# FP4 block in an order written out by hand, one PSUM tile for each gate product, and moved fillers in the attention passes

## The chip, the cores and the metric

The kernel runs on one core of one Trainium2 chip. The metric is the time of one execution on the device in microseconds (us), lower is better. Engines are named as in the profile: PE (TensorE, matrix products into PSUM), DVE (VectorE), ACT (ScalarE), POOL (GpSimd), SP (SyncE, which issues the DMAs).

## The reference

Two layers work on `x` of shape (8, 224, 512) with a context `ctx` of shape (8, 750, 512), all in float32. Each layer is a gated cross attention and a gated feed-forward block. Cut to what matters:

```python
x = x + tanh(g_xattn[0]) * xattn16(layernorm(x), ctx)      # 16 heads of 32
x = x + tanh(g_ffn[0])   * ternary_ffn(layernorm(x))       # 512 -> 2048 -> 512
x = x + tanh(g_xattn[1]) * xattn8(layernorm(x), ctx, mask) # 8 heads of 64, masked
x = x + tanh(g_ffn[1])   * fp4_ffn(layernorm(x))           # 512 -> 1408 -> 512

def bit_linear(x, w):             # ternary_ffn: two of these, with a convolution of
    return einsum(act_quant(x), weight_quant(w))   # three taps and silu between them

def fp4_quant_dequant(x):         # blocks of 16
    scale = max(|x|) / 6
    return nearest of (0, .5, 1, 1.5, 2, 3, 4, 6) to |x / scale|, * sign(x) * scale

def fp4_ffn(x):
    gate, y = fp4_linear(x, w_gate), fp4_linear(x, w_up)
    return fp4_linear(silu(gate) * y, w_down)
```

## The kernel before

The work is cut into sixteen passes, `n` from 0 to 15, and a block at the end. Passes 0 to 7 are the eight batches of the first layer's attention (`attention16`), passes 8 to 15 those of the second layer's (`attention8`). The FP4 feed-forward block (`ffn1`) then works on 14 tiles of 128 rows; tiles 0 and 1 have their hidden part computed inside pass 15 (`ffn1_head`), so the block computes the hidden part of tiles 2 to 13 and the output of all 14.

**Queues of pieces.** Matrix work that no pass waits for at once is written as generators that yield after every matmul or small group, each time with its cost on PE and on DVE: the keys and queries of the next pass (`keys_queries`), the values (`values`), the projections of the pass before (`project_out`, `ffn0_out`), the ternary feed-forward (`ffn0`), the FP4 quantization of the weights (`fp4_weights`, lines 959 to 974 and 1000) and of the activations (`fp4_steps`). `fill(us, queues)` issues pieces until that much PE time is covered; `pace(us, queue)` issues pieces until DVE has that much to do. `self.owed` is the PE time already covered beyond what was asked, `self.behind` the DVE time put behind.

**First layer.** A pass has sixteen slots of scores and maxima: scores in the PSUM tile `quad` (line 461), a maximum on DVE (line 468), and `fill(1.72)` for PE meanwhile. Then come twelve steps: scores again (429, 438), the exponential on ACT (504), filler of 2.05, DVE work of up to 4.0, in which a ternary product (813, into bank `t`) may lie, and the products with the values (515). A reciprocal and a product (524, 525) close each group of three steps. `diagonals` and `spread` (193, 201, 204) lay the ternary scale `bc` over the partitions ahead of the ternary products; line 821 takes a product out of bank `t` into `hp`.

**Second layer.** A pass has eight slots: scores (612), the masked maximum (623), the exponential (644), products with the values (575) and transposes of the weights (670, copied at 675). `divided` turns the row sums into reciprocals in steps: rows `stat` on DVE (586 to 411), their transposes (417) with a copy to `sT` (419), a product that spreads them (593, copied at 597), and a product on DVE (601). The transposes of the FP4 weights (1000, copied at 1018 or 1028), of `stat` and of the normalized rows `xn` (185, copied at 186) all go through the one buffer of PSUM bank `t`; keys (293, copied to `kT` at 302), queries, values and projections share the two buffers of bank `m`.

**FP4 block.** `ffn1_hidden` takes four chunks of 352 columns. For each, four matmuls make the gate product, ACT a tanh and DVE `gth` (1078), four more make the up product, and DVE multiplies (1080). Both products are halves of one PSUM tile, `ps_big`, of which there are two. `ffn1_in` loads a tile `xf`, normalizes it, quantizes it (POOL has the last step, 974) and transposes it into `xqT` (1055; copied by `evac`, in turn on ACT, line 89, and on DVE, line 91). `ffn1_out` transposes the quantized hidden row (1092, copied at 1093), multiplies with `wd` (1097) and stores (1109, 1110).

**Order.** `pin` makes PE, DVE and ACT follow the order in which the kernel's lines were traced. Here it is called ahead of the FP4 block, so the block's order is a scheduler's, and its lines only say what depends on what; a dependency is kept by tile, not by part of a tile.

## Time and profile before

| | |
|---|---|
| median of 3 runs | 2239.82 us (2235.03 to 2239.95) |
| the profiled execution | 2234.42 us, span 2232.6 us |
| PE busy | 2151.8 us, 96% |
| DVE busy | 1385.0 us, 62% |
| ACT busy | 699.2 us, 31% |
| POOL busy | 130.7 us, 6% |
| DMA queue of the program | 79.18 MB, 11.3% of 16 engines |
| first layer's passes 2 to 7 | 124 us each, PE busy 121.3 |
| second layer's passes 10 to 13 | 97 to 98 us each, PE busy 93.8 to 95.4 |
| FP4 block, 1829 to 2229 | 400 us, PE busy 391.4 |

A float32 matmul stands in the trace as two records, a float32 transpose as one. A group of records is given with its start, its length, the line and the tiles, and in brackets the idle time of the engine ahead of it with what ended it. Times inside a pass are from the span's start. The granted clock is the share of TensorE's full clock that the throttle let through.

### The profile page before, as it was taken

How to read it: one execution, taken by the hardware profiler on the slowest of the kernel's cores; microseconds unless marked ns; L12 is line 12 of the kernel's file. 1: busy time of each engine (PE TensorE's matmuls, PEld its weight loads, DVE VectorE, ACT ScalarE, POOL GpSimd, SP SyncE). 2: the span in 40 equal slices, each digit the busy share in tenths (PEclk: the TensorE clock that was granted, in tenths of full speed). 3: DMA queues.
4: the chain of work that ended last, by engine and by line, in shares of the span. 5: the costliest groups of instructions: out<-in, count | busy, mean ns of one | idle time of the engine just before them, and what ended most of it. 6: DMA issues, size and time to landing. Idle time of an engine off the chain costs nothing.

```text
span 2232.6 us, 33189 instructions
## 1 busy us (share of the span) xinstructions
PE 2151.8 (96%) x14062; PEld 1226.2 (55%) x14062; DVE 1385.0 (62%) x2618; ACT 699.2 (31%) x1173; POOL 130.7 (6%) x145
## 2 busy tenths in 40 slices
PE   7989899999999999999899999999999999999999
PEld 4444546364555546465656565665656555555554
DVE  3786767676766767773656565564523468666652
ACT  1222415151423325152543343343434321110111
POOL 0000000000000000000001010110000012111110
PEclk9999999999999999999999999999999999999999
DMA  6210010101000011101011212122110020000000
GB/s 218 67 38 29 1 45 2 31 15 30 16 18 29 7 39 39 63 2 63 3 38 57 63 28 64 41 67 66 37 36 15 9 85 10 5 20 19 19 5 19
DMA packets 48628, 81.30 MB, mean 36 GB/s; under 512 B 3296, under 2 KB 27616, under 8 KB 48352
## 3 DMA queue, kind: packets, MB, share of 16 engines
q1 hardware_dynamic: 48480, 79.18, 11.3%
q8 instruction: 110, 1.80, 0.3%
q14 instruction: 38, 0.31, 0.0%
HBM read 65.28 MB, written 13.89 MB: 35 GB/s over the span
## 4 chain that ended last, share of the span: by engine, by line
PE 84%; DVE 12%; ACT 2%; issue 1%; DMA 1%; SPq 0%; POOL 0%; ACTq 0%; DVEq 0%
PE ps_m L354 14%; PE ps_m L293 12%; PE ps_big L1066 7%; PE ps_pa L515 6%; PE ps_m L1097 6%; PE ps_m L378 5%; PE ps_quad L461 4%; PE ps_half L612 4%; PE ps_m L322 4%; PE ps_half L670 4%; PE ps_pa L575 4%; PE ps_quad L438 3%; PE ps_t L813 2%; DVE part L468 2%; PE ps_m L1066 2%; PE ps_quad L429 1%
## 5 line engine op out<-in xcount | busy, mean ns | idle before, releaser
L293 PE MATMUL ps_m<-cx,wk 128*128 128x375 f32 x1024 | 362.4, 487 | 10.0 <-DMA wk<-in_L_Wk 10.0
L354 PE MATMUL ps_m<-wv,cx 128*125 128x512 f32 x768 | 354.5, 602 | 0.0
L623 DVE CUSTOM_DVE_ANT_0 ps_half<-ps_half,mbias 112x750 f32<-112x750 f32 x128 | 121.1, 946 | 292.1 <-PE ps_half L612 291.8
L468 DVE TENSOR_REDUCE part<-ps_quad 112x4 f32<-112x1500 f32 x128 | 220.0, 1719 | 127.0 <-PE ps_quad L461 127.0
L293 PEld LDWEIGHTS ps_m<-cx,wk 128*128 128x128 f32 x1024 | 182.4, 191 | 110.8 <-issue 28.3
L354 PEld LDWEIGHTS ps_m<-wv,cx 128*125 128x125 f32 x768 | 136.1, 187 | 173.8 <-issue 168.8
L504 ACT ACTIVATE p<-ps_quad 125x1792 f32<-125x1792 f32 x96 | 159.7, 1664 | 198.8 <-PE ps_quad L438 198.8
L363 ACT COPY v<-ps_m 125x512 f32<-125x512 f32 x96 | 56.1, 585 | 439.0 <-PE ps_m L354 433.8
L1097 PE MATMUL ps_m<-wd,hqT 128*128 128x512 f32 x308 | 138.3, 595 | 3.8 <-ACT hqT L1093 3.1
L644 ACT ACTIVATE p<-ps_half,nm 112x750 f32<-112x750 f32 x128 | 113.1, 888 | 47.6 <-DVE nm L635 41.7
L675 ACT COPY p<-ps_half 125x672 f32<-125x672 f32 x128 | 85.8, 722 | 131.6 <-PE ps_half L670 131.6
L461 PE MATMUL ps_quad<-kT,qT 32*112 32x375 f32 x1024 | 115.3, 519 | 11.8 <-DVE part L468 11.8
L378 PE MATMUL ps_m<-wo,aT 128*112 128x512 f32 x256 | 120.4, 601 | 0.0
L1066 PE MATMUL ps_big<-wg,xqT 128*128 128x352 f32 x352 | 115.4, 463 | 1.8 <-DVE h L1080 1.4
L1066 PE MATMUL ps_big<-wu,xqT 128*128 128x352 f32 x352 | 113.7, 466 | 0.8 <-DVE gth L1078 0.8
L837 DVE SCALAR_TENSOR_TENSOR y<-hp,cw,y 128x224 f32<-128x224 f32 x256 | 109.5, 449 | 4.5
L322 PE MATMUL ps_m<-xnT,wq 128*128 128x224 f32 x512 | 107.9, 357 | 0.6 <-ACT xnT L186 0.6
L515 PE MATMUL ps_pa<-p,v 125*32 125x224 f32 x1536 | 93.3, 361 | 14.8 <-ACT p L504 14.8
L1077 ACT ACTIVATE gth<-ps_big 128x352 f32<-128x352 f32 x48 | 22.2, 463 | 257.2 <-PE ps_big L1066 234.1
L670 PE MATMUL ps_half<-ident,p 112*125 112x112 f32 x768 | 99.9, 280 | 0.0
L612 PE MATMUL ps_half<-kT,qT 64*112 64x375 f32 x512 | 98.5, 498 | 0.9 <-ACT p L675 0.9
L322 PEld LDWEIGHTS ps_m<-xnT,wq 128*128 128x128 f32 x512 | 93.7, 190 | 9.4 <-issue 5.3
(199 smaller groups left out, 2873.7 us busy)
## 6 DMA issues: line engine op xcount, KB each, us to landing
cx<-in_ctx SPq DMA_DIRECT2D x32, 750.0 KB, 4.3
wst<-in_w SPq DMA_DIRECT2D x16, 512.0 KB, 7.8
x<-in_x SPq DMA_DIRECT2D x8, 448.0 KB, 7.0
mid<-x SPq DMA_DIRECT2D x8, 448.0 KB, 3.1
x<-mid SPq DMA_DIRECT2D x8, 448.0 KB, 3.5
last<-x SPq DMA_DIRECT2D x8, 448.0 KB, 3.1
out<-yout SPq DMA_DIRECT2D x14, 256.0 KB, 2.0
wraw<-in_w_gate SPq DMA_DIRECT2D x11, 256.0 KB, 2.6
```

Source lines behind the costliest of these rows:

```text
L293: nc.tensor.matmul(pk, lhsT=self.w["wk"][:, k, g * 128 : (g + 1) * 128], rhs=job["cx"][c][:, k, :], start=k == 0, stop=k == KC - 1,)
L322: nc.tensor.matmul(pq[:, g - g0, :], lhsT=self.w["wq"][:, k, g * 128 : (g + 1) * 128], rhs=xnT[:, k, :], start=k == 0, stop=k == KC - 1,)
L354: nc.tensor.matmul(pv, lhsT=job["cx"][c][:, k, at : at + CP], rhs=self.w["wv"][:, k, :], start=k == 0, stop=k == KC - 1,)
L378: nc.tensor.matmul(po, lhsT=aT[:, g, i * TP : (i + 1) * TP], rhs=self.w["wo"][:, g, :], start=g == 0, stop=g == KC - 1,)
L461: nc.tensor.matmul(sc[:, h, :MH], lhsT=qT[r, g, i * TP : (i + 1) * TP], rhs=kT[g][r, c * MH : (c + 1) * MH], start=True, stop=True,)
L468: nc.vector.tensor_reduce(part[:, i, g, :, c], sc[:, :, :MH], AX.X, ALU.max)
L504: nc.scalar.activation(p, pw[:, :, : 2 * S], AF.Exp)
L515: nc.tensor.matmul(pa[r, which, :], lhsT=self.ones[:CP, r] if which else job["v"][j][:, col : col + 32], rhs=p[:, h, (j - j0) * S : (j - j ...
L612: nc.tensor.matmul(sc[h][:, c, :MH], lhsT=qT[r, g, i * TP : (i + 1) * TP], rhs=kT[g][r, c * MH : (c + 1) * MH], start=True, stop=True,)
L670: nc.tensor.transpose(pt[:, j // half, j % half * TP : (j % half + 1) * TP], p[:, h, j * CP : (j + 1) * CP], self.ident[:TP, :TP],)
L1066: nc.tensor.matmul(ps[:, :CW], lhsT=xqT[:, k, :], rhs=wt[:, k, c0 : c0 + CW], start=k == 0, stop=k == KC - 1,)
L1097: nc.tensor.matmul(po, lhsT=hqT[:, k, :], rhs=wd[:, k, :], start=k == 0, stop=k == NC1 - 1)
```

## The change

- `transposed` takes a bank: the transposes of the queries' rows go to `m` in place of `t` where the queries' pass is 8 or later.
- In `attention16` the first slot's filler is 2.9 in place of 1.72 (not in pass 0), and the filler of 2.05 is less by 0.8 where the piece that `pace` will issue next is a ternary product (`ahead`, `self.coming`).
- In `attention8` the transposes of `stat` at slot 4 are traced ahead of the FP4 pieces; in pass 15, from slot 2, `pace` asks for 2.5 in place of 3.5.
- The last steps of a pass's reciprocals (`rest`) are issued together with every second matmul of the next pass's values, in one piece, in place of a piece of their own behind it.
- `xqT` is always copied by ACT. In `ffn1_head` the second tile's `xqT` has a buffer of its own, and the steps of the next tile's `ffn1_in` come after every fourth matmul in place of every fifth.
- In the FP4 block gate and up product have a PSUM tile each (`big=4`), and the loop over tiles writes out the order: while a tile's hidden part runs, the next tile's `ffn1_in`, the quantization of the tile before and the output of the tile before that are placed between its matmuls. `pin` is called at the very end, so this order holds on PE, DVE and ACT.

```diff
-        pt = self.ps("t", [128, KC, TP], BF16 if half else F32)
+        pt = self.ps(bank, [128, KC, TP], BF16 if half else F32)
...
+    def ahead(self, us, queue):
+        return self.coming if queue and self.behind < us else 0
...
-            self.transposed(xnT, xn, i)
+            self.transposed(xnT, xn, i, "t" if n < B else "m")
...
-                        self.fill(1.72, early, late)
+                        self.fill(2.9 if n and (g, i, c) == (0, 0, 0) else 1.72, early, late)
...
-                self.fill(2.05, late)
+                self.fill(2.05 - self.ahead(4.0 if j0 + 2 < NKT else 0.5, beside), late)
...
+            if slot == 4:
+                next(first)
             if not soon:
                 self.pace(1.5, beside)
-            if slot == 4:
-                next(first)
...
-                self.pace(3.5, beside)
+                self.pace(3.5 if n + 1 < 2 * B or slot < 2 else 2.5, beside)
...
         self.spread(bc, diags)
+        self.coming = 0.8
...
+            self.coming = 0.8 if g + 1 < ng else 0
             yield (0.8 if g < ng else 0), dve, g < ng
...
-        self.evac(xqT, pt)
+        nc.scalar.copy(xqT, pt)
...
         transposes(0, 4, "th")
         transposes(4, 8, "t")
+        yield
+        transposes(8, NC1, "th")
+        yield
         po = self.ps("m", [TF, D])
-        products(0, 4)
-        transposes(8, NC1, "th")
-        products(4, NC1)
+        products(0, 5)
+        yield
+        products(5, NC1)
...
-        room = self.att.tile([128, KC, MH], F32, name="cx", bufs=2)
+        room, other = (self.att.tile([128, KC, MH], F32, name="cx", bufs=2) for _ in range(2))
...
+        xqTs = [h["xqT"], other, h["xqT"]]
...
-                if i % 5 == 2 and i < 25:
+                if i % 4 == 2 and i < 27:
                     yield next(ahead)
...
         def banks():
-            ps = self.ps("big", [TF, 2, 512])
-            return ps[:, 0, :], ps[:, 1, :]
+            return [self.ps("big", [TF, CW]) for _ in range(2)]
...
+                ahead = self.ffn1_in(pool, f + 1, xf, xn, xT, 2)
+            steps = quantized(last)
+            for i, _ in enumerate(
+                self.ffn1_hidden(
+                    xqT, h, lambda: pool.tile([TF, CW], F32, name="gth", bufs=2), banks
+                )
             ):
+                if f + 1 < NF and i in (1, 4, 6, 9, 12, 14):
+                    next(ahead)
+                if i in (10, 15, 17, 20, 22, 25):
+                    next(steps)
+                if i in (23, 27):
+                    next(out)
+            for _ in steps:
                 pass
+            waiting.append(self.ffn1_out(pool, f, x, h, wd))
+            next(out)
...
-                for k, cost in enumerate(values):
-                    yield cost
+                for k, (pe, dve) in enumerate(values):
                     if k % 2:
-                        yield next(ends, (0, 0))
+                        more = next(ends, (0, 0))
+                        pe, dve = pe + more[0], dve + more[1]
+                    yield pe, dve
...
-        self.pin()
...
-            self.psum_pool(last, big=2, th=1)
+            self.psum_pool(last, big=4, th=1)
...
             self.ffn1(self.pool(last, "ffn1", side="right"), wd)
+            self.pin()
```

More of the change, by code (lines that the diff above doesn't have):

```diff
@@ L176, in normed, with transposed @@
         return xn
-    def transposed(self, dst, src, i):
+    def transposed(self, dst, src, i, bank="t"):
         nc = self.nc
         half = src.dtype == BF16
-        pt = self.ps("t", [128, KC, TP], BF16 if half else F32)
+        pt = self.ps(bank, [128, KC, TP], BF16 if half else F32)
         ident = self.ident16 if half else self.ident
@@ L1145, in quantized @@
                 yield from self.fp4_steps(work, part, part, part.shape[1])
+        other = other.rearrange("p k m -> p (k m)")[:, :D].rearrange("p (k t) -> p k t", k=KC)
+        xqTs = [h["xqT"], other, h["xqT"]]
         for f in range(2):
-            ahead = self.ffn1_in(there, f + 1, h["x"][f + 1], h["xn"], h["xqT"], 1)
+            ahead = self.ffn1_in(there, f + 1, h["x"][f + 1], h["xn"], xqTs[f + 1], 1)
             for i, cost in enumerate(
                 self.ffn1_hidden(
-                    h["xqT"],
+                    xqTs[f],
                     h["h"][f],
@@ L1169, in quantized @@
             for c0 in range(0, HID1, QW):
-                self.fp4(pool, h[:, c0 : c0 + QW], h[:, c0 : c0 + QW], QW, 2)
+                yield from self.fp4_steps(pool, h[:, c0 : c0 + QW], h[:, c0 : c0 + QW], QW, 2)
         def banks():
-            ps = self.ps("big", [TF, 2, 512])
-            return ps[:, 0, :], ps[:, 1, :]
+            return [self.ps("big", [TF, CW]) for _ in range(2)]
         x, h, xqT = self.head["x"], self.head["h"], self.head["xqT"]
-        waiting = [(0, x[0], h[0]), (1, x[1], h[1])]
@@ L1178, in ffn1 @@
-        x = x[2]
-        quantized(h[1])
+        waiting = [self.ffn1_out(pool, f, x[f], h[f], wd) for f in range(2)]
+        x, last = x[2], h[1]
         for f in range(2, NF):
+            out = waiting.pop(0)
             h = pool.tile([TF, HID1], F32, name="h", bufs=3)
-            for _ in self.ffn1_hidden(
-                xqT, h, lambda: pool.tile([TF, CW], F32, name="gth", bufs=2), banks
-            ):
-                pass
-            waiting.append((f, x, h))
+            if f + 1 < NF:
+                xf = pool.tile([TF, D], F32, name="xf", bufs=5)
+                xn = pool.tile([TF, D], F32, name="xn1", bufs=2)
+                xT = pool.tile([128, KC, TF], F32, name="xqT1", bufs=2)
+                ahead = self.ffn1_in(pool, f + 1, xf, xn, xT, 2)
[4 more added lines that the diff above has]
+                )
+            ):
+                if f + 1 < NF and i in (1, 4, 6, 9, 12, 14):
[5 more added lines that the diff above has]
+            for _ in steps:
+                pass
+            waiting.append(self.ffn1_out(pool, f, x, h, wd))
+            next(out)
@@ L1187, in ffn1 @@
             if f + 1 < NF:
-                x = pool.tile([TF, D], F32, name="xf", bufs=5)
-                xn = pool.tile([TF, D], F32, name="xn1", bufs=2)
-                xqT = pool.tile([128, KC, TF], F32, name="xqT1", bufs=2)
-                for _ in self.ffn1_in(pool, f + 1, x, xn, xqT, 2):
-                    pass
-            quantized(h)
-            self.ffn1_out(pool, *waiting.pop(0), wd)
-        for tile_ in waiting:
-            self.ffn1_out(pool, *tile_, wd)
+                for _ in ahead:
+                    pass
@@ L1200, in run @@
+                x, xqT = xf, xT
+            else:
+                for _ in quantized(h):
+                    pass
+                next(waiting[0])
+            for _ in out:
+                pass
+            last = h
+        first, second = waiting
+        next(first)
+        next(first)
+        next(second)
+        for _ in first:
+            pass
+        next(second)
+        for _ in second:
+            pass
     def run(self):
@@ L1202, in run @@
         self.setup()
-        self.owed, self.behind, self.jobs, self.w = 0, 0, {}, {}
+        self.owed, self.behind, self.coming, self.jobs, self.w = 0, 0, 0, {}, {}
         self.copy = self.nc.scalar.copy
```

## The prediction

> **What bounds the kernel now.** I read the page's busy times and its chain first, then the list of waits for TensorE alone, then the order in time around each wait.

> ```profile
> PE 2151.8 (96%) x14062; PEld 1226.2 (55%) x14062; DVE 1385.0 (62%) x2618; ACT 699.2 (31%) x1173; POOL 130.7 (6%) x145
> PE 84%; DVE 12%; ACT 2%; issue 1%; DMA 1%; SPq 0%; POOL 0%; ACTq 0%; DVEq 0%
> ```

> TensorE is busy 96% and is the chain. Its work is not changed, so only its waits can be won: 2232.6 - 2151.8 = 81 us, 10 of them the first load. The waits, as total, times, longest:

> ```profile
> PE ps_pa L515 <- ACT p L504: 14.8, 11, 1.9
> PE ps_quad L461 <- DVE part L468: 11.8, 16, 2.1
> PE ps_t L185 <- ACT wsome L1028: 2.5, 4, 0.7
> PE ps_m L1066 <- DVE wv L1078: 2.4, 2, 2.2
> PE ps_t L417 <- DVE hp L821: 2.2, 1, 2.2
> ```

> They are many, short and regular, so each place is looked at once and counted.

> **First layer, passes 1 to 7.** TensorE at the end of pass 2 (start, us, what; in brackets the idle time before it):

> ```profile
> 390.91 0.90 PE L293 MATMUL ps_m<-cx,wk 128*128 128x375 f32 x2
> 392.83 0.96 PE L515 MATMUL ps_pa<-p,v 125*32 125x224 f32 x16 [1.03 <-ACT p L504]
> ...
> 394.49 0.90 PE L461 MATMUL ps_quad<-kT,qT 32*112 32x375 f32 x8
> 395.31 1.93 PE L919 MATMUL ps_t<-w,hs 128*112 128x512 bf16 x8
> 398.29 0.90 PE L461 MATMUL ps_quad<-kT,qT 32*112 32x375 f32 x8 [1.04 <-DVE part L468]
> ```

> Filler ran out: one key matmul (two records, 0.63) stood where the exponential takes 1.66. Then the next pass's first maximum (1.71) came behind the reciprocal and product (1.56 + 0.39) with 1.93 of filler. In the built order of the changed kernel four key matmuls leave the early steps and two of them stand in the last one (three matmuls, 1.89, cover 1.66), and the first slot has twenty `L919` matmuls (4.3) instead of eight. Both waits go: -1.03 - 1.04. Given back: at step 1 the ternary product waits for `bc`, copied behind the exponential at 332.99 to 333.33 in pass 2; with 0.63 less ahead of it, its wait of 0.19 becomes 0.82 (+0.63). And one slot has two key matmuls (1.26) where a value and a key matmul stood (1.49), whose wait of 0.27 grows by 0.23. Net -1.2 in each of passes 2 to 7, -7.1. In pass 1 the wait of 2.10 at 152.4 and one of 0.62 at 206.7 are covered, 0.63 is given back, and the last steps stay short of filler: -2.5 (between 0 and -4).

> Edit against: the queries' transposes take bank `m` from `n >= B`, but the queries of layer 1's first pass run inside pass 7. There a key group has just ended in `m`, and the next needs its buffer: two buffers, transposes in the other. The copy `kT` comes behind the exponential, a tanh and two `y` on ACT and ended at 965.37, while the next key matmul started at 963.85. It will wait 1.5 us, and 1.7 at the second transposes: +3.2 (0 if ACT is early). Layer sum: -7.1 - 2.5 + 3.2 = -6.4.

> **Second layer, passes 8 to 14.** TensorE in pass 10:

> ```profile
> 1281.28 0.66 PE L1000 MATMUL ps_t<-ident,wq 128*128 128x128 f32 x4
> 1282.61 0.26 PE L417 MATMUL ps_t<-ident,stat 112*128 112x112 bf16 x2 [0.67 <-ACT wg L1018]
> ...
> 1292.36 0.66 PE L1000 MATMUL ps_t<-ident,wq 128*128 128x128 f32 x4
> 1293.69 0.60 PE L185 MATMUL ps_t<-ident,xn 112*128 112x112 f32 x4 [0.68 <-ACT wg L1018]
> ```

> One bank `t` is handed from the FP4 transposes to the next user through an ACT copy. A wait costs its idle time and about 0.2 of a weight load that no longer hides: end to end 0.88 to 0.99 where a transpose takes 0.11. Eight `L185` go to `m`, where the key group before them was copied during the scores: 8 x 0.86 = -6.9. Five `L593` now stand ahead of the scores and of the FP4 transposes: 5 x 0.80 = -4.0. Five `L417` stand ahead of `L1000` (once `L919`); but `L1000` then waits for the copy `sT`, 0.34 instead of 0.58: about -0.25 each, -0.5 where the wait was 0.84, -1.2 in all. In pass 8 the 2.2 of `L417` becomes about 0.4 for `sT` and 0.2 for `hp` at the next product (-1.4); its transposes lose their 1.56 wait for `hp`, but the key matmul after them waits for `kT`, copied at 1098.22 behind two `y` (+1.0), and another by 0.3. Sum -12.1 (from -7, if every freed wait turns into another copy's, to -16).

> **Pass 15.**

> ```profile
> 1795.11 2.53 PE L1066 MATMUL ps_m<-wu,wq 128*128 128x352 f32 x8
> 1799.84 3.69 PE L1066 MATMUL ps_m<-wg,wq 128*128 128x352 f32 x6 [2.20 <-DVE wv L1078]
> ```

> ```profile
> 1800.00:1804.00 4.00, 4.00 (x18) 2.23 (x20) 2.31 (x6) 0.00 (x0) 0.00 (x0) 0.60 0.00 0
> ```

> Won: the 2.18 at 1783.45 (`xqT` copied on DVE behind a queue; now on ACT, into its own buffer, five matmuls earlier) and the 0.88 of `L417` at 1819.79. Lost: ahead of the same gate product `L1078` the DVE order now holds three FP4 steps of 1.85 and three of 1.28 where it held 2.46, so 2.2 becomes 3.1; the one at 1771 grows by 0.8; at the end the last up product stands behind the transposes, so `L417` waits for `h` (0.7) and the `stat` rows (1.4), 2.1 in all; and since `pace` asks for less, 5.6 of FP4 steps instead of 1.5 stand between those rows and `L601`, which the output projection needs: 2.5 more. Against 5.3 before, 8.5 after, less 0.7 that the earlier start gives: +2.5 (from -3 to +6).

> The last row shows that a wait can cost twice: the granted clock was 0.60 in these 4 us, and six records took 3.69 where 5 x 0.296 + 0.459 = 1.94: 1.75 more. I charge the 1.75 after 3.1 as after 2.2, so it cancels. [...]

> **The FP4 block from 1828.5 to 2228.9.**

> ```profile
> 2018.68 3.12 PE L1066 MATMUL ps_big<-wg,xqT 128*128 128x352 f32 x10
> 2021.73 2.63 PE L1066 MATMUL ps_big<-wu,xqT 128*128 128x352 f32 x8
> 2024.20 2.93 PE L1066 MATMUL ps_big<-wg,xqT 128*128 128x352 f32 x8
> ```

> Eight records back to back take 2.53: one takes 0.459, so each further one (2.53 - 0.459) / 7 = 0.296. Longer groups hide waits of 0.1 to 0.4: the up product writes the tile that DVE's `gth` reads, and waits for it. Dense, from rows: 768 records x 0.296 = 227.3; 308 of `L1097` x 0.429 ((6.17 - 0.592)/13) = 132.1; 198 transposes x 0.109 = 21.6; together 381.0, against 400.4 now: 19.4 of waits. With a tile for each product and the order written out, a tile is 64 x 0.296 + 22 x 0.429 + 15 x 0.109 = 30.0 (now 31.6). I went through one such tile from its first matmul: the gate product of chunk 0 is on DVE by 5.8 and its bank wanted at 9.5; chunk 1 by 11.4 against 15.1; `xn` by 14.4 against 24.5; DVE has 21 us of work in 30. The transposed halves are copied (0.59) behind 2.37 of gate product; `xqT` behind six `L1097`. `xf` is asked for a tile ahead; SP's order is the old one but for one store ahead of the first `xf`, and POOL's follows DVE's. The copies of `xqT` that leave DVE (0.68) cost ACT 0.58 each, which is busy 12% there: nothing. The last tile's FP4 is done at 33.5, its transposes' turn is 35.2. Of the 19.4 I take 18.5; half if DVE slips.

> **Sum.** -6.4 - 12.1 + 2.5 - 18.5 = -34.5. The profiled execution took 2234.42 (span 2232.6), the median of the three runs 2239.82, of which one was 2235.03. So 2199.9 on the profiled time, and 2202.5 with half of the 5.4 between.

> **Rivals.** *Waits in the block only move* (12%): with the order fixed, nothing fills in when DVE or POOL is late, and half of its 19.4 stays: 2212. For it: POOL's 1.39 and 1.06 follow DVE's; against it, the margins above. *Waits in the attention only move* (12%): filler is conserved, so a covered wait may open elsewhere; 0 for the first layer and -7 for the second: 2214. *Nothing* (3%): gains and new waits cancel, 2237; the built order speaks against it. *Slower by the clock* (3%): half-clock windows of 3.41 us, each at 1.75. The block has 110 such windows; from (34.5 + 6.7) / 1.75 = 24 of them the kernel is slower; at half, 2202.5 + 96 = 2299. Against it: the present block cycles its banks with 30 short waits and no granted window under 1.00 after 1803. [...] *Slower by the queue* (2%): `xf`'s statistics stand ahead of chunk 0's gate product on DVE. There are 3.6 us of room beyond the 2.9 of a landing; from 3.5 us lost in each of 12 tiles on top the kernel is slower, at 4.5 it is 2256.

> **Numbers.** My forecast has the other 68%. Low end: each term near its better bound, -46: 2188. High end: -18.5 and the median's 5.4, 2221, which takes in the two moving rivals. A measurement tells about 0.3% (6.7 us) from no change: faster 0.92, same 0.03, slower 0.05.

> **What would show it.** Right: no `L185 <- ACT wg`, no `L515 <- ACT p` after pass 1; the block's matmuls within 383 us; `L813 <- ACT bc` up to 0.8. Also the losses: `L293` waiting for `kT` in passes 7 and 8, `L378` for `L601`, `L1066 <- DVE L1078` near 3. Wrong: tiles over 31 us, or clock rows under 1.00 in the block.

## The result: 2207.31 us, 1.4% faster

The changed kernel took 2207.31 us (median of four runs, 2203.95 to 2208.25), the kernel before 2239.12 us beside it: a ratio of 0.9859, 95% interval 0.9842 to 0.9876, or 32 us. The forecast was 2202.5 us. The two profiled executions are 26.2 us apart (2234.42 and 2208.25; spans 2232.6 and 2206.5). By part, in us, a pass being counted from its first matmul of scores to that of the next pass in the two traces:

| part | forecast | measured |
|---|---|---|
| start, passes 0 and 1 | -2.5 | +1.5 |
| passes 2 to 6 | -6.0 | -4.8 |
| pass 7 | +2.0 | +2.0 |
| pass 8 | -0.1 | +2.2 |
| passes 9 to 14 | -12.0 | -11.3 |
| pass 15 | +2.5 | +3.5 |
| FP4 block | -18.5 | -19.2 |
| sum | -34.5 | -26.2 |

The forecast's parts are rounded, so they add up to -34.6.

The page of the changed kernel, its busy times and its chain (line numbers are those of each run's own kernel: `L520` of the changed kernel is `L515` of the kernel before):

```profile
PE 2144.9 (97%) x14062; PEld 1231.4 (56%) x14062; DVE 1387.0 (63%) x2611; ACT 702.1 (32%) x1180; POOL 130.2 (6%) x145
PE 88%; DVE 9%; ACT 1%; issue 1%; DMA 0%; POOL 0%; SPq 0%; ACTq 0%; DVEq 0%
```

TensorE is a larger part of the chain. Outside its busy time there are now 2206.5 - 2144.9 = 62 us, 19 fewer. Busy time fell too, by 7, with the same work (14062 records in both): a record that waits a little inside a group is counted as busy, as the prediction said of the block's longer groups (eight records took 2.63 and 2.93 there, and take 2.53 now). The waits of TensorE (total, times, longest):

```profile
PE ps_pa L520 <- ACT p L509: 8.0, 5, 1.9
PE ps_quad L465 <- DVE part L472: 6.0, 8, 3.3
PE ps_t L819 <- ACT bc L204: 5.7, 7, 0.8
PE ps_m L297 <- ACT kT L306: 4.5, 3, 2.7
PE ps_m L1073 <- DVE wv L1085: 4.1, 2, 3.1
```

The exponential's wait (once 14.8) is left only in passes 0 and 1, the maximum's (once 11.8) is half, and `L185 <- ACT wsome` (once 2.5) is gone. The last three rows are the losses named in the forecast: 0.8 for `bc`, `kT` in passes 7 and 8, 3.1 for `L1085`.

The end of pass 2 on TensorE, where two waits of 1.03 and 1.04 stood:

```profile
391.32 2.16 PE L297 MATMUL ps_m<-cx,wk 128*128 128x375 f32 x6
393.41 0.96 PE L520 MATMUL ps_pa<-p,v 125*32 125x224 f32 x16
...
395.89 3.66 PE L926 MATMUL ps_t<-w,hs 128*112 128x512 bf16 x16
399.39 1.03 PE L926 MATMUL ps_pa<-w,hs 128*112 128x512 bf16 x4
400.35 0.90 PE L465 MATMUL ps_quad<-kT,qT 32*112 32x375 f32 x8
```

Three key matmuls, not one, cover the exponential, and twenty `L926` matmuls cover the reciprocal and the maximum. No row has a bracket.

The block, first as a row of windows (length, busy time of PE, PEld, DVE, ACT and POOL, granted clock, DMA share, GB/s), then two groups of one tile:

```profile
1821.00:2203.00 382.00, 381.68 (x1276) 224.29 (x1274) 253.23 (x451) 49.12 (x101) 54.22 (x48) 1.00 0.06 22
```

```profile
1946.24 2.53 PE L1073 MATMUL ps_big<-wg,xqT 128*128 128x352 f32 x8
1948.61 2.53 PE L1073 MATMUL ps_big<-wu,xqT 128*128 128x352 f32 x8
```

Every group of eight records has the back-to-back length of 2.53, and each of the tiles 2 to 12 takes 30.02 us, for a dense sum of 30.0. The block has no listed wait.

### The profile page after: what moved, and what is told of

It is laid out like the page before. It is cut to its first block, busy times and chain, and to the rows that moved or that the text cites. A ratio compares the mean times of both kernels' runs of the same rounds, so it can differ in the third digit from the quotient of the medians.

```text
span 2206.5 us, 33210 instructions
## 1 busy us (share of the span) xinstructions
PE 2144.9 (97%) x14062; PEld 1231.4 (56%) x14062; DVE 1387.0 (63%) x2611; ACT 702.1 (32%) x1180; POOL 130.2 (6%) x145
## 3 DMA queue, kind: packets, MB, share of 16 engines
q1 hardware_dynamic: 48480, 79.18, 11.4%
## 4 chain that ended last, share of the span: by engine, by line
PE 88%; DVE 9%; ACT 1%; issue 1%; DMA 0%; POOL 0%; SPq 0%; ACTq 0%; DVEq 0%
PE ps_m L358 16%; PE ps_m L297 11%; PE ps_big L1073 10%; PE ps_pa L520 6%; PE ps_m L1105 6%; PE ps_m L382 5%; PE ps_quad L465 5%; PE ps_m L326 4%; PE ps_half L617 4%; PE ps_half L675 4%; PE ps_pa L580 4%; PE ps_quad L442 3%; PE ps_t L819 2%; PE ps_m L1073 2%; PE ps_quad L433 1%; PE ps_t L926 1%
## 5 line engine op out<-in xcount | busy, mean ns | idle before, releaser
L297 PEld LDWEIGHTS ps_m<-cx,wk 128*128 128x128 f32 x1024 | 182.2, 191 | 119.3 <-issue 31.3
L520 PE MATMUL ps_pa<-p,v 125*32 125x224 f32 x1536 | 93.8, 362 | 8.0 <-ACT p L509 8.0
L580 PEld LDWEIGHTS ps_pa<-p,v 125*64 125x64 f32 x1536 | 76.1, 139 | 33.3 <-issue 30.2
```

The costliest lines, as they stand in the source:

```text
L297: nc.tensor.matmul(pk, lhsT=self.w["wk"][:, k, g * 128 : (g + 1) * 128], rhs=job["cx"][c][:, k, :], start=k == 0, stop=k == KC - 1,)
L520: nc.tensor.matmul(pa[r, which, :], lhsT=self.ones[:CP, r] if which else job["v"][j][:, col : col + 32], rhs=p[:, h, (j - j0) * S : (j - j ...
L580: nc.tensor.matmul(banks["pa"][r, g % 2, i * TP : (i + 1) * TP], lhsT=job["v"][j][:, col : col + 64], rhs=pT[:, h, j * TP : (j + 1) * TP], ...
```

## What the changed kernel's trace added: half-clock windows

In the profile of before, the granted clock was at half in two windows of 3.41 us; after, in five. Two rows of windows of the changed kernel (the clock is the third number from the end):

```profile
264.30:267.80 3.50, 3.50 (x40) 1.85 (x44) 2.20 (x3) 0.00 (x0) 0.00 (x0) 0.51 0.00 0
1063.00:1066.50 3.50, 3.50 (x22) 2.17 (x22) 1.96 (x6) 0.79 (x2) 0.69 (x1) 0.51 0.00 0
```

The second follows a wait that the change did not touch. TensorE there, after and before:

```profile
1062.38 0.37 PE L185 MATMUL ps_t<-ident,xq 112*128 112x112 bf16 x4 [2.40 <-DVE xq L796]
1062.59 2.37 PE L297 MATMUL ps_m<-cx,wk 128*128 128x375 f32 x4
```

```profile
1063.58 0.37 PE L185 MATMUL ps_t<-ident,xq 112*128 112x112 bf16 x4 [2.39 <-DVE xq L791]
1063.78 1.49 PE L293 MATMUL ps_m<-cx,wk 128*128 128x375 f32 x4
```

The same wait of 2.4 us was followed by full clock in one execution and by half clock in the other. In the profile's clock records the starts of all windows of one trace lie whole multiples of 3.413 us apart, which is also the length of one window (35, 269, 482 and 488 after the first in the changed kernel's: 144.86, 264.33, 1063.05, 1790.09, 1810.57; 485 in that of before: 144.32, 1799.78): they lie on a grid. The grid doesn't start with the kernel: its first line lies 1.5 us behind the span's start in this trace and 1.0 in that of before. I laid the grid over the twelve traces of this case and took TensorE's idle time in each interval, from the first record of the clock on (15.2 us behind the span's start in this trace, 14.6 in that of before). After 39 intervals with 1.88 us or more idle, 38 times the next was at half clock; after 28 with 1.80 to 1.87, 9 times; after 7658 with less, 6 times, of which 4 were the second interval of a double window and the other two had 1.70 and 1.77. In the traces of before and after alone these are 4 of 4, 3 of 6 and 0 of 1280. The wait of 2.4 above lay whole in one interval after (2.40), and in two before (1.31 and 1.07). By these counts, as an estimate, a wait between 1.9 and 3.4 us is hit when about 1.9 of it falls in one interval, which is chance.

A hit costs up to 3.41 / 2 = 1.7 us by the clock of 0.50 in such a window: pass 8 takes 113.96 with the window and 112.31 without it in another kernel (head_mended, below) with the same pass. It also goes with the spread of the runs. The 29 runs of before beside the three groups of experiments had a mean granted clock of 1.000 (one run, 2232.0 us), 0.998 (14 runs, 2233.9 to 2236.3), 0.997 (7, 2237.5 to 2238.8) and 0.996 (7, 2239.5 to 2240.6). A mean lower by 0.004 is 9 us of lost clock in 2240, and the times are 8 to 9 us apart. The profiled execution of before had two windows, of which that at 144.3 cost nothing, since TensorE waits for DVE right behind it: 2.10 us at 152, and 3.73 in split_alone (below), which has the same passes and no window there. That of the changed kernel had five, the one at 144.9 nearly as free. Three more at 1.7 are 5.1 us: at equal windows the profiles differ by 26.2 + 5.1 = 31.3 us, as the medians do. Without these windows three rows of the table above would be about -0.1 (start), +0.5 (pass 8) and +1.8 (pass 15).

## The experiments

Each kernel below ran beside the kernel before, and its ratio is against those runs. The changed kernel wasn't run again beside them, and the kernel before took 2235.45, 2234.59 and 2238.01 us (medians) in the three groups, where it took 2239.12 in the result. Differences of whole times from 2207.31 are therefore uncertain by a few us. The passes of the traces are surer: passes 10 to 13 agree within 0.03 us between runs whose code is the same there.

**The block's two halves.** First the separate tiles alone, in the kernel before:

```diff
         def banks():
-            ps = self.ps("big", [TF, 2, 512])
-            return ps[:, 0, :], ps[:, 1, :]
+            return [self.ps("big", [TF, CW]) for _ in range(2)]
...
-            self.psum_pool(last, big=2, th=1)
+            self.psum_pool(last, big=4, th=1)
```

> The kernel before with one edit: a PSUM tile for each gate and up product of the FP4 block; the block's order stays a scheduler's. My theory (the up product writes the tile that gth reads, and waits for it): most of the block's 19.4 us of waits go, the block falls from 400 to about 387 us and the kernel by 13, to about 2226. Rival (what costs is the order in which DVE and TensorE take the block's steps): the block stays within 3 us of 400, and the kernel at 2239.

2233.12 us, ratio 0.9976 (0.9964 to 0.9989): the means of the runs are 5 us apart, of the 13 expected. The block took 395.4 instead of 400.5, with a double half-clock window in it that cost 3.4. At full clock that is 392.0, or 8.5 of the block's 19.2; the three of ten runs with a mean clock of 0.998 took 2226.1 to 2227.2, about 8 less than before at that clock, and the others had 0.995 or 0.996. Two tiles in turn take 61.1 us, where they took 63.1 before and 60.0 in the changed kernel. What TensorE waits for there from 1841 on:

```profile
PE ps_t L1092 <- DVE xqT L91: 2.2, 5, 0.8
PE ps_t L1055 <- POOL xn L974: 1.6, 1, 1.6
PE ps_m L1097 <- ACT hqT L1093: 1.6, 4, 0.7
```

The waits for `gth` and `h` (2.2 in this stretch of before) are nearly gone; those of the transposes and their copies stay. In all the listed waits are not fewer (7.6, and 6.9 before), so what was won lay inside the groups of matmuls: TensorE's busy time in the block fell from 392.1 to about 384.5 us at full clock. Both theories hold a part. What takes the block from 392.0 to 381.3 is not fully separated: the changed kernel has the written order and also copies `xqT` always on ACT, and the 2.2 in the first row are for a copy on DVE. No run has one of the two without the other. Then the written order with the shared tile, in the changed kernel (the diff above the other way round):

> The changed kernel with one edit: gate and up product are again halves of one PSUM tile, of which there are two; the written order stays. My theory (the shared tile costs): in the written order nothing but three of four gaps with no other work stands between a gate product and its up product, so the up product waits for the copy on ACT and for gth, about 0.2 + 0.46 + 0.05 + 0.52 = 1.2 us, at 36 of 48 chunks: the block takes 381 + 43 = 424 us, more than the 400 of before, and the kernel about 2250. Rival (the order is what was won): the block stays within 3 us of 381 and the kernel at 2207.

2303.49 us, ratio 1.0302 (1.0287 to 1.0317): slower than before, by more than expected. The block took 477.2, which is 77 more than before and 96 more than in the changed kernel. One total of waits, and two groups of a tile:

```profile
PE ps_big L1073 <- DVE gth L1085: 71.4, 48, 6.5
```

```profile
1920.40 2.63 PE L1073 MATMUL ps_big<-wu,xqT 128*128 128x352 f32 x8 [2.45 <-DVE gth L1085]
...
1927.39 2.63 PE L1073 MATMUL ps_big<-wu,xqT 128*128 128x352 f32 x8 [0.78 <-DVE gth L1085]
```

All 48 up products wait, not 36. Two of a tile's four wait the expected 1.1 to 1.2, one 2.45, where quantization steps, the last of 0.89, stood ahead of `gth` on DVE, and one 0.78. Besides 71.4 of waits, 48 weight loads of about 0.2 that no longer hide (a load of this product takes 0.19 in the trace of before) make 10 by my estimate, and eight half-clock intervals in the block, at 1.7 each, 14: 95 of the 96 us. The written order is only good here with a tile for each product. Last, the same block with the order pinned only up to it:

```diff
+        self.pin()
         prep.close()
...
             self.ffn1(self.pool(last, "ffn1", side="right"), wd)
-            self.pin()
```

> The changed kernel with the order pinned only up to the FP4 block: the block keeps its separate tiles and the text of its loop, but a scheduler orders DVE, ACT and TensorE. TensorE's order is the same but for one group of transposes; on DVE steps of the quantization come ahead of some gth. My theory (separate tiles carry the gain): the block stays within 4 us of 381, the kernel within 2207 to 2211. Rival (the pinned order on DVE carries it): half of the 19.4 comes back, the block takes about 390 and the kernel 2217.

2208.24 us, ratio 0.9875 (0.986 to 0.989), block 380.8: no difference. The gain comes from separate tiles, the copies on ACT and the order in which the loop is written; pinning that order adds nothing. The steps that the scheduler moves on DVE are covered: TensorE has no listed wait in the block there either.

**The queries' rows.**

```diff
-            self.transposed(xnT, xn, i, "t" if n < B else "m")
+            self.transposed(xnT, xn, i, "t")
```

> The changed kernel with one edit: the transposes of the queries' rows go to bank t in every pass, as before. By my reckoning: pass 7 is 3.0 us shorter (no key matmul waits for kT), pass 8 about 1.1 shorter (2.66 + 0.18 of waits for kT go, the wait of 1.56 for hp returns), and passes 9 to 14 get eight waits of about 0.86 back, 6.9 us. Sum +2.8, about 2210. Rival (the bank made no difference in passes 9 to 14, the reciprocals' steps did): 4 us faster than the changed kernel, about 2203.

2210.44 us, ratio 0.9888 (0.9871 to 0.9904), 3.1 more than the changed kernel (2.8 expected). Passes 10 to 13 are 1.66 to 1.79 longer, 6.9 together as forecast, pass 14 0.8; pass 7 is 3.0 shorter, pass 8 1.6 (110.75 for 112.31, both without a window). So bank `m` is worth 7.7 us in passes 10 to 14 and costs 4.6 in passes 7 and 8, in these rows of the changed kernel:

```profile
962.09 0.90 PE L297 MATMUL ps_m<-cx,wk 128*128 128x375 f32 x2 [1.70 <-ACT kT L306]
```

```profile
1098.10 2.80 PE L297 MATMUL ps_m<-cx,wk 128*128 128x375 f32 x8 [2.66 <-ACT kT L306]
```

**The reciprocals' steps.**

```diff
-                for k, (pe, dve) in enumerate(values):
+                for k, cost in enumerate(values):
+                    yield cost
                     if k % 2:
-                        more = next(ends, (0, 0))
-                        pe, dve = pe + more[0], dve + more[1]
-                    yield pe, dve
+                        yield next(ends, (0, 0))
...
-            if slot == 4:
-                next(first)
             if not soon:
                 self.pace(1.5, beside)
+            if slot == 4:
+                next(first)
```

> The changed kernel with the last steps of the reciprocals in a piece of their own again, and the transposes of stat at slot 4 behind the FP4 pieces again. My theory: in passes 9 to 14 five L598 wait 0.8 each and five L421 0.25 more: passes 10 to 13 take 95.7 instead of 94.7 us, the kernel 5 more, 2212. Rival (the transposes' bank, which the run before this one showed to be worth 1.8 in each of passes 10 to 13, is all of the second layer's gain): passes 10 to 13 stay at 94.7 and the kernel at 2207.

2214.1 us, ratio 0.9906 (0.9886 to 0.9927), 6.8 more. Passes 10 to 13 took 95.64, 95.65, 95.53 and 96.11, passes 9 to 13 together 3.7 more, in waits of about 0.67 of `L598` and `L421` for the copies `wg`, `wu` and `wsome`. With the 7.7 above this makes up the 11.3 of passes 9 to 14. The rival falls. The rest of the 6.8 is not the order in passes 9 to 14: pass 8 is 1.1 longer, where `L421` waits 2.2 for `hp` again, and pass 7 is 1.6 longer with a half-clock window at 961.6, both in the profiled run.

**The first layer's filler.**

```diff
-    self.fill(2.9 if n and (g, i, c) == (0, 0, 0) else 1.72, early, late)
+    self.fill(1.72, early, late)
...
-    self.fill(2.05 - self.ahead(4.0 if j0 + 2 < NKT else 0.5, beside), late)
+    self.fill(2.05, late)
```

> The changed kernel with the first layer's filler as before (1.72 in the first slot, 2.05 in every step). My theory (the filler covers two waits of 1.0 in each pass): passes 2 to 6 take 123.8 instead of 122.87 us, 0.95 more each, pass 7 as well, and passes 0 and 1 together stay within 1 us of their 238.2 apart from half-clock windows: +6, about 2213. Rival (the changed filler is what made pass 1 longer by 1.5): passes 2 to 7 as above, but passes 0 and 1 together fall to 236.9: +4.5.

2214.79 us, ratio 0.9905 (0.9887 to 0.9922), 7.5 more. Passes 2 to 6 take 123.83, 0.96 more each, and pass 7 1.2 more; pass 8 has a double half-clock window. Passes 0 and 1 together took 236.95, the rival's figure, against 238.21 in the changed kernel. But the window at 264 makes 1.65 of the latter, so the filler didn't make pass 1 longer: at equal windows it brought 0.4. It covered the wait of 2.10 near 152, but ran out earlier: near 201 a normalization that waits for POOL came ahead of a maximum on DVE, and the wait of 1.32 there became 3.31. On DVE and then TensorE, in the changed kernel:

```profile
198.86 0.55 DVE L173 TENSOR_SCALAR xn<-x,mv,rstd 112x512 f32<-112x512 f32 x1 [0.80 <-POOL rstd L168]
199.32 1.72 DVE L472 TENSOR_REDUCE part<-ps_quad 112x4 f32<-112x1500 f32 x1
```

```profile
201.09 0.90 PE L465 MATMUL ps_quad<-kT,qT 32*112 32x375 f32 x8 [3.31 <-DVE part L472]
```

**Pass 15.**

```diff
-                if i % 4 == 2 and i < 27:
+                if i % 4 == 3 and i < 28:
...
+        self.finish([rest, self.project_out(2 * B - 1)])
         self.finish(beside)
-        self.finish([rest, self.project_out(2 * B - 1)])
...
         def rest():
-            yield next(second)
             product(*before)
             yield 1.3, 0
+            yield next(second)
```

The last edit holds for pass 15 alone.

> The changed kernel with three edits at pass 15: the steps of the next tile's input come after every fourth matmul, but behind gth and the product with it instead of ahead of them; the last reciprocals issue their product with the values first and the transposes of stat behind it; what is left of the FP4 pieces is issued behind the output projection instead of ahead of it. My theory (DVE takes FP4 steps ahead of what TensorE waits for): the wait of 3.1 for L1085 falls to about 1.9, the 1.9 for stat to 0.3, the 1.3 for aT to 0, and a half-clock window goes with them: 3.5 to 6 us less, about 2203. Rival (these waits only move to the first tiles of the block): head, projection and tile 2 together stay within 1 us.

2198.9 us, ratio 0.9836 (0.982 to 0.9853), 8.4 less, where 3.5 to 6 were expected. Head and projection took 73.0 instead of 81.4, and tile 2 still 30.02: nothing moved into the block. The changed kernel first, then this one:

```profile
1788.66 2.52 PE L1073 MATMUL ps_m<-wg,cx 128*128 128x352 f32 x6 [3.12 <-DVE wv L1085]
...
1809.63 0.27 PE L421 MATMUL ps_t<-ident,stat 112*128 112x112 bf16 x2 [1.91 <-DVE stat L411]
...
1816.18 1.11 PE L382 MATMUL ps_m<-wo,aT 128*112 128x512 f32 x2 [1.34 <-DVE aT L606]
```

```profile
1785.07 2.04 PE L1078 MATMUL ps_m<-wg,cx 128*128 128x352 f32 x6 [1.61 <-DVE wv L1090]
...
1804.42 0.27 PE L421 MATMUL ps_t<-ident,stat 112*128 112x112 bf16 x2 [0.32 <-DVE stat L411]
```

The waits fall by 1.5 + 1.6 + 1.3, and both half-clock windows behind them (3.4) are gone in this profile, where the expectation counted one. The three edits were made together, so no run shows what each is worth.

**The clock by itself.**

```diff
+ short = self.fill(2.05 - self.ahead(4.0 if j0 + 2 < NKT else 0.5, beside), late)
+ if n < 2 and short > 1.2:
+     idle = self.ps("m", [128, MH])
+     for k in range(2):
+         nc.tensor.matmul(idle, lhsT=self.w["wv"][:, k, :128],
+                          rhs=self.w["wv"][:, k, :MH], start=k == 0, stop=k == 1)
```

Here `fill` returns how much it left uncovered.

> The changed kernel with two matmuls, whose result is not used, in each place at the end of passes 0 and 1 where TensorE waits 1.85 us for the exponential with no filler left. By my theory of the clock (the granted clock halves for 3.41 us when TensorE was idle for 1.85 us or more within one interval of a 3.413 us grid) no half-clock window follows these waits, which shrink to about 0.6, and nothing else changes: passes 0 and 1 take 236 instead of 238.2 to 239.4 us, the mean clock is 0.001 higher and the kernel is 1 to 3 us faster than 2207. Rival (the windows come by chance, whatever the waits): windows as often as before at the end of passes 0 and 1.

The four waits fell from 1.85 to 0.40, no window followed them, and passes 0 and 1 took 236.3 us. But the kernel took 2209.07 (ratio 0.9875, 0.9856 to 0.9895): no gain. The profiled run (2204.07) had a mean clock of 0.998 and the other three 0.996, so these had more windows; the longer waits near 200, 1062, 1098 and 1786 are still there to be hit, but which were is not recorded. The time doesn't bear the expectation out; the places of the windows do, weakly (of the intervals with 1.80 to 1.87 idle only 9 of 28 were hit).

**Both repairs together.** The three edits at pass 15, the rows in bank `t` up to the queries of pass 9, and the filler of 2.9 from pass 2 on:

```diff
-            self.transposed(xnT, xn, i, "t" if n < B else "m")
+            self.transposed(xnT, xn, i, "t" if n < B + 2 else "m")
...
-    self.fill(2.9 if n and (g, i, c) == (0, 0, 0) else 1.72, early, late)
+    self.fill(2.9 if n > 1 and (g, i, c) == (0, 0, 0) else 1.72, early, late)
```

> The changed kernel with the three edits at pass 15 of the run head_mended, the queries' rows of passes 8 and 9 (which run inside passes 7 and 8) through bank t, and the first slot's longer filler from pass 2 on only. By the passes of the other runs: head_mended's 2198.9, less 3.0 in pass 7 (no key matmul waits for kT), less about 1.1 in pass 8 (2.66 + 0.18 of waits for kT go, 1.56 for hp returns), nothing in pass 1: about 2195. Rival (the rows in bank t wait longer than the keys did): pass 8 longer than 112.3, and 2197 or more.

2195.16 us, ratio 0.981 (0.9797 to 0.9824), the fastest of all. Pass 7 took 122.85 (3.0 less), pass 8 112.36 with a window in it, and pass 1 gained nothing. The same with the unused matmuls:

> The kernel mended with the two unused matmuls in each uncovered wait for the exponential of passes 0 and 1. By my theory of the clock no half-clock window follows these four waits, nor any in passes 0 and 1 but behind the wait of 2.1 near 152: with half of the four waits hit in other runs, 1.7 us each where TensorE sets the pace, about 1 to 2 us less than mended. Rival (windows come by chance): the same time as mended within 0.5 us and windows at these places.

2197.04 us, ratio 0.9818 (0.9804 to 0.9831): 1.9 more in the median than without them, with ranges that overlap, where 1 to 2 less were expected. There is no window at the four places in the profile, but the unused matmuls bring nothing.

## Why the forecast held, and where it was off

- **The FP4 block** (-18.5, measured -19.2): dense at 30.02 a tile, and the margins on DVE held. Neither half of the change does it: separate tiles alone took 8.5 off the block at full clock (5 us of the kernel's time as the runs came out), and the written order with the shared tile made the block 77 longer. That the waits in the block only move did not happen, nor did the clock fall anywhere in it: with four banks in turn, here in float32 with 352 columns, the granted clock is 1.00 over the block's 382 us.
- **Second layer** (-12.1, measured -9.2): eight `L185` were put at 6.9, and passes 10 to 14 showed 7.7; the reciprocals' steps were put at 4.0 + 1.2 and showed 3.6. The term that failed is pass 8's "+1.0" for the key matmul behind the transposes: `kT` came 2.66 late there, and without a window pass 8 is 0.5 longer than before, not 0.1 shorter. The window at 1063 makes 1.65 more.
- **First layer**: the working of passes 2 to 6 is right but for a wait of 0.34 of the transposes for `hp` at 366 that was not counted (-0.96 for -1.2; six times 1.2 is also 7.2 and not 7.1). The +3.2 of pass 7 came as 1.70 + 1.64. The "-2.5" of pass 1 failed: its own rows give 2.10 + 0.62 - 0.63 = 2.1, and the covered wait opened again 50 us later, behind DVE. This is the moving rival, true in one pass only.
- **Pass 15** (+2.5, measured +3.5): 3.1 was 3.12, 2.1 was 1.91, 2.5 was 1.34. What failed is "so it cancels": the half clock behind the 3.1 was charged, but the 1.9 for `stat` was hit too, 1.7 more.
- **The clock.** The forecast charged it once, as a fixed price of one wait. In the twelve traces it was a chance: half clock followed 9 of 28 intervals with 1.80 to 1.87 us idle, and 38 of 39 with more. This took 5.1 us of the 34.5 in the two profiles. By the 29 runs it also explains the 5.4 between the profiled time and the median: times near 2239.8 all came with a mean clock of 0.996, where the profiled run had 0.998. The forecast halved this difference without a reason, so it is in part luck that the median was missed by only 4.8 us, where the difference of the profiles was missed by 8.3.

## What to carry to other kernels

When an order is written out by hand, every tile that two engines share has to be split as far as the order needs it: dependencies were kept by tile (with the shared one all 48 up products waited for `gth`, 71.4 us in all), and in the same order the block takes 381.3 us with the split and 477.2 without it, against 400.5 before. A step that DVE takes ahead of what TensorE waits for was dear at the end of pass 15, where no filler is left (4.4 us of waits went with the three edits there); moving it behind cost nothing in the block that follows (tile 2 still takes 30.02). Compare profiles pass by pass, and count the half-clock windows of both before any difference of a few us is explained.
